# Tile norms in two parts an output apart, and requests in front of a tile's sums in GpSimd's queue

## The chip, the cores and the metric

The kernel runs on one core of a Trainium2 chip. The metric is the device time of one execution in microseconds (us); of a kernel that was run several times the median is given. The engines are TensorE (PE in the profile, its weight loads PEld), VectorE (DVE), ScalarE (ACT), GpSimd (POOL) and SyncE (SP). Each works off its own queue in order, and they wait for each other through semaphores.

## The reference, cut to what matters

Two layers of a gated transformer block on x of shape (4, 512, 256), all in float32. Each layer adds gated cross attention to a context and then a gated feed-forward part. Layer 0 has attention with a time decay and a feed-forward part with ternary weights. Layer 1 has attention with ReLU projections and then a feed-forward part with four experts, and that last part is where the change lies:

```
x = x + tanh(g_xattn[0]) * L0_attention(layernorm(x), ctx)
x = x + tanh(g_ffn[0])   * L0_ffn(layernorm(x))
x = x + tanh(g_xattn[1]) * L1_attention(layernorm(x), ctx)
x = x + tanh(g_ffn[1])   * L1_ffn(layernorm(x))

def L1_ffn(t):                       # t: (2048, 256)
    expert = argmax(t @ W_router)    # one of 4 for each token
    h = gelu(t @ W1[expert] + b1[expert])          # (2048, 1024)
    y = h @ Wo + bo + t
    return layernorm(y, eps=1e-12) * ln_gamma + ln_beta
```

## The kernel before, in words

Attention, routing and the first feed-forward part are worked in units whose order a small planner writes out; all of that stays as it is. The 2048 tokens of the last part are sorted by expert into 16 tiles of 128 tokens, so that a tile needs the weights of one expert only (the last three tiles, 13 to 15, mix two experts each and need two). The lists that say which token goes to which tile are made four times, each time with more of the batch routed: list 2 gives tiles 9 to 12, the mixed list tiles 13 to 15. The instructions that make a list run mostly on VectorE, with a collection on TensorE (`pidT`, line 999, then `pid`, line 1008) and a memset on GpSimd (`tid`, line 959) between them.

The code that the change touches runs after the last attention unit, at about 706 us. For each tile j:

- `fetch_rows(j)` (line 1037) and `fetch_weights(j)` (line 1053) are indirect transfers that GpSimd requests: the tile's 128 token rows, normed and not normed side by side (`xr`, 512 floats a row), and about 1 MB of expert weights (`wg`). A request needs the token or weight numbers of the list, and a free place in its pool.
- `turn_tile(j)`, "t j" in the queue below (line 1065): two transposes on TensorE, copied out by ScalarE.
- `hidden_half(j, f2, k)`, "h j" (line 1090): the hidden products on TensorE, GELU on ScalarE (line 1116); in the mixed tiles a second pass with other weights and a masked copy on VectorE (line 1106).
- `output_tile(j)`, "o j": y = row + bias on VectorE (line 1282), eight products into `pyf` on TensorE (line 1285), y = y + pyf on VectorE (line 1289).
- `norm_tile(j)`: statistics on VectorE (lines 1294, 1296, 1299), the power -1/2 of the variance on GpSimd (`rstd_y`, line 1300), a first multiply on VectorE (line 1301), three small instructions that refine the power (lines 1302 to 1306), and the last multiply and add (line 1307).
- `put_tile(j)` (line 1312): an indirect transfer, requested by GpSimd, that writes the tile's rows to their tokens' places in the output. Each put waits until the put before it has landed.

The order of all engines' queues in this part is the order in which the loop over `queue` calls these functions:

```
h4 o0 o1 o2 t5 o3 h5 t6 o4 h6 t7 o5 h7 t8 o6 h8 o7 t9 o8 t10 h9 h10 t11 o9 h11 t12 o10 h12
t13 o11 h13 t14 o12 h14 t15 o13 h15 o14 o15
```

`steps` hangs the making of list 2 and of the mixed list onto entries of it: after o1 the transposes of the last batch's routing, after o2 its products, after o3 its logits, after h5 ranks and list 2 up to `row_d`, after o4 the selections (`sel_d`, line 986) and weight rows, after o5 the collection, after h7 the tokens (line 1014) and a first part of the mixed list (`mixes`), after o6 and h8 two more, after o7 the mixed places, after o8 the mixed tiles (with the memset), after h9 the mixed selections, after h10 their collection, after o9 the mixed tokens. In each entry the order was: products; the steps; for an output its norm and the put of the tile before; and then the requests of `rows_at` and `weights_at`.

Of the kernel before, what the change touches and what calls it, by code (L numbers as in the profile page):

```python
# [11 lines left out]
F32 = mybir.dt.float32  # L12
U32 = mybir.dt.uint32
AF = mybir.ActivationFunctionType
ALU = mybir.AluOpType
# [4 lines left out]
P = 128  # L20
B, S, D = 4, 512, 256
H, DK = 16, 16
NT = S // P
# [8 lines left out]
TT = B * NT  # L32
# [19 lines left out]
def flamingo_kernel(ctx: ExitStack, tc: tile.TileContext, t: dict, out: bass.AP):  # L52
    nc = tc.nc
# [7 lines left out]
    sml = ctx.enter_context(tc.tile_pool(name="sml", bufs=4))  # L61
    ps = ctx.enter_context(tc.tile_pool(name="ps", bufs=8, space=PSUM))

    def bank_psum(name):
        return ps.tile([P, 512], F32, tag="bank", name=name)
# [36 lines left out]
    bo0, b20, bo1, gam1, bet1 = (rows[:, i, :] for i in range(5))  # L102
# [6 lines left out]
    def weight_place(name):  # L109
        return wts.tile([P, NC * FF + NF], F32, tag="wff", name=name)  # L110
# [21 lines left out]
    act = att.__enter__()  # L132
# [895 lines left out]
    xg, wg = {}, {}  # L1028

    def fetch_rows(j):  # L1030

        have = max(n for n, first in LISTS if first <= j or n == LISTS[0][0]) * S
        if j in (3, *range(LISTS[1][1], TT)) and made["behind"]:
            xg[j] = act.tile([P, 2 * D], F32, tag="xr", name=f"xr{j}", bufs=5)
        else:
            xg[j] = wts.tile([P, 2 * D], F32, tag="xg", name=f"xg{j}", bufs=4)
        nc.gpsimd.indirect_dma_start(  # L1037
            out=xg[j], out_offset=None, in_=rows_d[0:have, :],
            in_offset=bass.IndirectOffsetOnAxis(ap=token[:, j : j + 1], axis=0),
            bounds_check=have - 1, oob_is_err=False,  # L1040
        )


    def weights_of(j):
        return (j,) if j < T_ONE else (2 * j - T_ONE, 2 * j - T_ONE + 1)

    def fetch_weights(j):

        if j < T_AHEAD or (j - T_AHEAD) % 5 < 2:
            wg[j] = weight_place(f"wg{j}")  # L1050
        else:
            wg[j] = act.tile([P, NC * FF + NF], F32, tag="wg", name=f"wg{j}", bufs=3)
        nc.gpsimd.indirect_dma_start(  # L1053
            out=wg[j], out_offset=None, in_=t["w1e"],
            in_offset=bass.IndirectOffsetOnAxis(ap=wrow[:, j : j + 1], axis=0),
            bounds_check=NE * P - 1, oob_is_err=False,
        )

    made["behind"] = False
    xs, hs, ys, biases = {}, {}, {}, {}  # L1060
# [9 lines left out]
    def hidden_half(j, f2, k=0):  # L1070


        w1 = wg[weights_of(j)[k]]
        w = w1[:, 0 : NC * FF].rearrange("p (c f) -> p c f", c=NC)
        b1 = w1[:, NC * FF :]
        if j < T_AHEAD:
            ha = wts.tile([P, S], F32, tag="h", name=f"ha{j}{f2}", bufs=8)
            if f2 == 0:
                biases[j] = sml.tile([P, NF], F32, tag="b1", name=f"b1_{j}")
                nc.gpsimd.tensor_copy(biases[j], b1)  # L1080
        else:
            ha = act.tile([P, S], F32, tag="ha", name=f"ha{j}{f2}{k}", bufs=8)
            biases[j] = b1
        ha = ha.rearrange("p (f n) -> p f n", n=P)
        if k == 0:
            hs[j, f2] = ha
        ph = bank_psum(f"pg{j}{f2}{k}").rearrange("p (f n) -> p f n", n=P)
        for f in range(NF // 2):
            for c in range(NC):
                nc.tensor.matmul(  # L1090
                    ph[:, f, :], lhsT=w[:, c, ts(f2 * NF // 2 + f, P)], rhs=xs[j][:, c, :],
                    start=(c == 0), stop=(c == NC - 1),
                )
        if j < T_AHEAD:
            (nc.scalar.copy if j < T_AHEAD - 1 else nc.vector.tensor_copy)(ha, ph)
        else:
            activated(j, f2, ph, ha)
        if k == 1:

            m = j - T_ONE  # L1100
            if f2 == 0:
                masks[m] = act.tile([P, P], U32, tag="mask", name=f"mask{m}")
                nc.vector.tensor_scalar(
                    masks[m], made["from_one"], lim[:, m : m + 1], None, ALU.is_gt
                )
            nc.vector.copy_predicated(
                hs[j, f2], masks[m].unsqueeze(1).to_broadcast([P, NF // 2, P]), ha
            )
# [141 lines left out]
    for u in range(-NT, n_units):  # L1250
# [22 lines left out]
        if u in totals:  # L1273
            job, i = totals[u]
# [2 lines left out]
    assert not any(c["steps"] for c in chains), [c for c in chains if c["steps"]]  # L1277


    def output_tile(j):  # L1280
        y = ys[j] = act.tile([P, D], F32, tag="y", name=f"y{j}", bufs=4)
        nc.vector.tensor_tensor(y, xg[j][:, 0:D], bo1, ALU.add)
        py = bank_psum(f"pyf1_{j}")[:, 0:D]
        for f in range(NF):
            nc.tensor.matmul(  # L1285
                py, lhsT=hs[j, f // 4][:, f % 4, :], rhs=wo1[f // 4][:, f % 4, :],
                start=(f == 0), stop=(f == NF - 1),
            )
        nc.vector.tensor_tensor(y, y, py, ALU.add)

    def norm_tile(j):
        y = ys[j]
        st = sml.tile([P, 6], F32, tag="st", name=f"st_y{j}")
        nc.vector.bn_stats(st, y)
        mv = sml.tile([P, NT, 2], F32, tag="mv", name=f"mv_y{j}")
        nc.vector.bn_aggr(mv[:, 0, :], st)

        var, rstd, fix = (sml.tile([P, NT], F32, tag=v, name=f"{v}_y{j}") for v in ("var", "rstd", "fix"))
        nc.vector.tensor_scalar(var[:, 0:1], mv[:, 0, 1:2], 1e-12, None, ALU.add)
        nc.gpsimd.tensor_tensor(rstd[:, 0:1], var[:, 0:1], power[:, 0:1], ALU.pow)  # L1300
        nc.vector.scalar_tensor_tensor(y, y, mv[:, 0, 0:1], gam1, ALU.subtract, ALU.mult)
        nc.vector.scalar_tensor_tensor(
            fix[:, 0:1], rstd[:, 0:1], var[:, 0:1], rstd[:, 0:1], ALU.mult, ALU.mult
        )
        nc.vector.tensor_scalar(fix[:, 0:1], fix[:, 0:1], -0.5, 1.5, ALU.mult, ALU.add)
        nc.vector.tensor_tensor(rstd[:, 0:1], rstd[:, 0:1], fix[:, 0:1], ALU.mult)
        nc.vector.scalar_tensor_tensor(  # L1307
            y, y, rstd[:, 0:1], xg[j][:, D : 2 * D], ALU.mult, ALU.add
        )

    def put_tile(j):
        nc.gpsimd.indirect_dma_start(  # L1312
            out=out.rearrange("b s d -> (b s) d"),
            out_offset=bass.IndirectOffsetOnAxis(ap=token[:, j : j + 1], axis=0),
            in_=ys.pop(j), in_offset=None, bounds_check=B * S - 1, oob_is_err=False,
        )
# [5 lines left out]
    for f2 in range(2):  # L1322
# [5 lines left out]
    act = ctx.enter_context(tc.tile_pool(name="moe", bufs=2))  # L1328
# [12 lines left out]
    steps = {  # L1341
        ("o", 1): [turn3], ("o", 2): [products3], ("o", 3): [logits3],
        ("h", 5): [ranks3, lists, token_places, by_tile], ("o", 4): [*sels, by_expert],
        ("o", 5): [collected], ("h", 7): [tokens, mixes[0]], ("o", 6): [mixes[1]],
        ("h", 8): [mixes[2]], ("o", 7): [mixed_places], ("o", 8): [mixed_tiles],
        ("h", 9): mixed_sels, ("h", 10): [mixed_collected], ("o", 9): [mixed_tokens],
    }
# [9 lines left out]
        queue.insert(queue.index(place), item)  # L1357
    queue += [("o", TT - 2), ("o", TT - 1)]

    rows_at = {("h", 4): [6], ("o", 0): [7], ("o", 1): [8], ("o", 6): [9, 10], ("o", 7): [11]}  # L1360
    weights_at = dict(rows_at)
    for j in range(8, TT - 4):
        rows_at["o", j] = [j + 4]
    weights_at |= {
        ("o", 8): [12, 13], ("o", 9): [14], ("o", 10): [15], ("h", 12): [16], ("o", 11): [17],
        ("h", 13): [18],
    }
    for kind, j in queue:
        if kind == "h":
            for k in range(len(weights_of(j))):  # L1370
                for f2 in range(2):
                    hidden_half(j, f2, k)
        elif kind == "t":
            turn_tile(j)
        else:
            if j < 3:
                for f2 in range(2):
                    activated(j + 1, f2)
            output_tile(j)
        for job in steps.pop((kind, j), ()):  # L1380
            job()
        if kind == "o":
            norm_tile(j)
            if j > 0:
                put_tile(j - 1)
        for i in rows_at.pop((kind, j), ()):
            fetch_rows(i)
            if i in weights_at.get((kind, j), ()):
                fetch_weights(i)
        for i in weights_at.get((kind, j), ()):  # L1390
            if i not in wg:
                fetch_weights(i)
    put_tile(TT - 1)
    assert not steps


# [73 lines left out]
```

## Time and profile before

| what | value |
|---|---|
| median of 3 runs | 847.55 us (846.2 to 848.15) |
| the profiled execution | 847.92 us, its span 845.8 us |
| TensorE (PE) busy | 811.0 us, 96% of the span |
| VectorE (DVE) busy | 569.1 us, 67% |
| ScalarE (ACT) busy | 422.2 us, 50% |
| GpSimd (POOL) busy | 270.9 us, 32% |
| mean granted TensorE clock | 0.991 |

The span runs from the first to the last instruction of the profiled execution; 2.1 us of its time lie around it. In a row of the timeline stand the start in us from the span's start, the time that the row took, engine and line, the operation, what it writes and reads, a count, and in brackets how long the engine sat idle before it and what ended that wait. A wait for several semaphores is put down to the one that came last in the profile, which need not be the one that mattered. Rows of the waits give the engine and line that waited, what ended it, the sum in us, how often, and the longest.

### The profile page before, as it was taken

How to read it: one execution, taken by the hardware profiler on the slowest of the kernel's cores; microseconds unless marked ns; L12 is line 12 of the kernel's file. 1: busy time of each engine (PE TensorE's matmuls, PEld its weight loads, DVE VectorE, ACT ScalarE, POOL GpSimd, SP SyncE). 2: the span in 40 equal slices, each digit the busy share in tenths (PEclk: the TensorE clock that was granted, in tenths of full speed). 3: DMA queues.
4: the chain of work that ended last, by engine and by line, in shares of the span. 5: the costliest groups of instructions: out<-in, count | busy, mean ns of one | idle time of the engine just before them, and what ended most of it. 6: DMA issues, size and time to landing. Idle time of an engine off the chain costs nothing. (4 is left out here: it accounts for less than half of the span.)

```text
span 845.8 us, 13576 instructions
## 1 busy us (share of the span) xinstructions
PE 811.0 (96%) x5220; PEld 452.4 (53%) x5220; DVE 569.1 (67%) x1272; ACT 422.2 (50%) x884; POOL 270.9 (32%) x439
## 2 busy tenths in 40 slices
PE   6999999999999999999999999999999999898994
PEld 3444444535464345544474444554545557787993
DVE  6768868766857776568737676558688654786443
ACT  2475555653645453455426474346556667332341
POOL 5536445524333243321101120002103314526522
PEclk9999999999999999999999999999999999999997
DMA  8200000000001000000000010000104422707730
GB/s 314 68 1 1 1 1 1 2 1 1 1 1 38 1 1 1 1 26 1 1 1 26 1 46 6 1 1 1 51 2 150 144 96 89 255 13 243 258 138 19
DMA packets 17712, 42.27 MB, mean 50 GB/s; under 512 B 2033, under 2 KB 12017, under 8 KB 15217
## 3 DMA queue, kind: packets, MB, share of 16 engines
q0 software_dynamic: 5104, 27.34, 9.3%
q1 hardware_dynamic: 12128, 13.54, 4.7%
q8 instruction: 41, 0.67, 0.3%
q10 hardware_dynamic: 416, 0.54, 0.2%
q14 instruction: 23, 0.18, 0.1%
HBM read 35.13 MB, written 6.29 MB: 49 GB/s over the span
## 5 line engine op out<-in xcount | busy, mean ns | idle before, releaser
L512 DVE TENSOR_REDUCE m<-pm 128x1 f32<-128x512 f32 x512 | 316.7, 681 | 109.0 <-PE psc L498 106.5
L527 ACT ACTIVATE p<-psc 128x512 f32<-128x512 f32 x512 | 267.1, 602 | 151.8 <-PE psc L498 149.4
L498 PE MATMUL psc<-q,k 32*128 32x512 f32 x1024 | 278.7, 623 | 0.2 <-DVE h L676 0.2
L498 PE MATMUL pm<-k,q 32*128 32x512 f32 x1024 | 262.7, 616 | 1.5 <-ACT q L485 0.9
L530 POOL TENSOR_TENSOR p<-p,dec 128x256 f32<-128x256 f32 x128 | 93.7, 736 | 178.7 <-ACT p L527 178.7
L498 PEld LDWEIGHTS pm<-k,q 32*128 32x128 f32 x1024 | 92.9, 184 | 84.1 <-issue 50.2
L498 PEld LDWEIGHTS psc<-q,k 32*128 32x128 f32 x1024 | 106.3, 184 | 52.0 <-issue 25.9
L555 PE MATMUL po<-p,v 128*32 128x512 f32 x1024 | 116.5, 595 | 1.9 <-DVE m L512 1.9
L555 PEld LDWEIGHTS po<-p,v 128*32 128x32 f32 x1024 | 31.7, 109 | 81.8 <-issue 60.8
L1090 PE MATMUL pg<-xs,wg 128*128 128x128 f32 x608 | 71.6, 276 | 0.4 <-DVE m L512 0.4
L1090 PEld LDWEIGHTS pg<-xs,wg 128*128 128x128 f32 x608 | 69.8, 192 | 3.8 <-DVE m L512 1.4
L623 POOL TENSOR_TENSOR x<-x,o 128x256 f32<-128x256 f32 x14 | 10.2, 727 | 174.4 <-DVE o L616 131.7
L1116 ACT ACTIVATE ha<-pg,wg 128x128 f32<-128x128 f32 x120 | 34.2, 368 | 53.0 <-PE pg L1090 53.0
L668 PE MATMUL ph<-xTf,w1q 128*128 128x512 f32 x128 | 60.0, 605 | 0.0
L1285 PE MATMUL pyf<-wo,ha 128*128 128x256 f32 x256 | 59.3, 387 | 0.0
L383 PE MATMUL py_f<-w2q,h 128*128 128x256 f32 x256 | 57.2, 381 | 0.0
L561 ACT COPY oT<-po 128x512 f32<-128x512 f32 x32 | 18.7, 584 | 77.1 <-PE po L555 77.1
L383 PEld LDWEIGHTS py_f<-w2q,h 128*128 128x128 f32 x256 | 48.0, 190 | 9.3 <-DVE m L512 3.0
L1285 PEld LDWEIGHTS pyf<-wo,ha 128*128 128x128 f32 x256 | 48.7, 195 | 6.4
L455 PE MATMUL pk<-cT,wk 128*128 128x512 f32 x68 | 35.3, 644 | 7.2 <-DMA cT<-in_ctxT_dram 7.2
L668 PEld LDWEIGHTS ph<-xTf,w1q 128*128 128x128 f32 x128 | 22.6, 189 | 30.4 <-issue 18.2
L388 DVE SCALAR_TENSOR_TENSOR x<-py_f,tg,x 128x512 f32<-128x512 f32 x8 | 6.0, 751 | 42.8 <-PE py_f L383 42.8
(256 smaller groups left out, 816.5 us busy)
## 6 DMA issues: line engine op xcount, KB each, us to landing
x<-in_x_dram SPq DMA_DIRECT2D x4, 512.0 KB, 8.7
rows_d<-xn_f SPq DMA_DIRECT2D x4, 512.0 KB, 3.0
rows_d<-x SPq DMA_DIRECT2D x4, 512.0 KB, 3.4
cT<-in_ctxT_dram SPq DMA_DIRECT2D x3, 512.0 KB, 9.5
w1q<-in_w_dram SPq DMA_DIRECT2D x1, 1024.0 KB, 9.0
w2q<-in_w_dram SPq DMA_DIRECT2D x1, 1024.0 KB, 11.3
wo<-in_wo_dram SPq DMA_DIRECT2D x2, 512.0 KB, 3.8
rows<-in_rows_dram SPq DMA_DIRECT2D x1, 640.0 KB, 9.2
```

The lines of the kernel that those rows point to most:

```text
L383: nc.tensor.matmul(py[:, n, :], lhsT=operand(c, n0 + n), rhs=w[:, c, :], start=(c == 0), stop=(c == chunks - 1),)
L455: nc.tensor.matmul(pp, lhsT=attn_w[layer][w][:, c, ts(tt, P)], rhs=src[:, c, :], start=(c == 0), stop=(c == NC - 1),)
L498: nc.tensor.matmul(out_, lhsT=lhs[r, ts(n, P)], rhs=rhs[r, :], start=True, stop=True)
L512: nc.vector.tensor_reduce(m[:, n, 2 * pair + i, r : r + 1], pm[i], AX.X, ALU.max)
L527: nc.scalar.activation(p[:, i, :], psc[i], AF.Exp, scale=SCALE)
L530: nc.gpsimd.tensor_tensor(d, d, dec.unsqueeze(1).to_broadcast([P, 2, P]), ALU.mult)
L555: nc.tensor.matmul(po[i * HP : (i + 1) * HP, :], lhsT=v_sb[b % 2][0][:, kt, c0 : c0 + HP], rhs=ps_exp[NT * s + kt, i // 2][:, i % 2, :], s ...
L561: nc.scalar.copy(pos[s], po)
L668: nc.tensor.matmul(ph, lhsT=w1q[:, c, ts(f, P)], rhs=st["xT"][:, c, :], start=(c == 0), stop=(c == NC - 1),)
L1090: nc.tensor.matmul(ph[:, f, :], lhsT=w[:, c, ts(f2 * NF // 2 + f, P)], rhs=xs[j][:, c, :], start=(c == 0), stop=(c == NC - 1),)
L1116: nc.scalar.activation(ha[:, f, :], (ha if src is None else src)[:, f, :], AF.Gelu, bias=biases[j][:, fa : fa + 1],)
L1285: nc.tensor.matmul(py, lhsT=hs[j, f // 4][:, f % 4, :], rhs=wo1[f // 4][:, f % 4, :], start=(f == 0), stop=(f == NF - 1),)
```

## The change

`norm_tile` is cut in two. `sum_tile(j)` holds both additions, the statistics, the power and the first multiply; `norm_tile(j)` holds the refining and the last multiply. An output's entry now runs: products, then requests of rows and weights, then the steps, then `sum_tile(j)`, then `norm_tile(j - 1)` and `put_tile(j - 2)`. For the last two tiles the second part comes directly behind the first, with its own put; tile 13's second part and puts 12 and 13 come after h15. Before, both additions stood ahead of the entry's steps in VectorE's queue; now they stand behind them.

The requests move too: rows 9 are asked for right after the tokens of list 2 (in h7) and weights 9 ahead of them, rows 13 right after the mixed tokens (in o9), and all others ahead of their entry's sum, so ahead of its power and put in GpSimd's queue. The pool of rows has 7 places instead of 5, that of y 5 instead of 4.

```diff
-            xg[j] = act.tile([P, 2 * D], F32, tag="xr", name=f"xr{j}", bufs=5)
+            xg[j] = act.tile([P, 2 * D], F32, tag="xr", name=f"xr{j}", bufs=7)
...
     def output_tile(j):
-        y = ys[j] = act.tile([P, D], F32, tag="y", name=f"y{j}", bufs=4)
-        nc.vector.tensor_tensor(y, xg[j][:, 0:D], bo1, ALU.add)
-        py = bank_psum(f"pyf1_{j}")[:, 0:D]
+        py = pys[j] = bank_psum(f"pyf1_{j}")[:, 0:D]
...
-        nc.vector.tensor_tensor(y, y, py, ALU.add)
-
-    def norm_tile(j):
-        y = ys[j]
+    def sum_tile(j):
+        y = ys[j] = act.tile([P, D], F32, tag="y", name=f"y{j}", bufs=5)
+        nc.vector.tensor_tensor(y, xg[j][:, 0:D], bo1, ALU.add)
+        nc.vector.tensor_tensor(y, y, pys.pop(j), ALU.add)
         st = sml.tile([P, 6], F32, tag="st", name=f"st_y{j}")
         nc.vector.bn_stats(st, y)
         mv = sml.tile([P, NT, 2], F32, tag="mv", name=f"mv_y{j}")
         nc.vector.bn_aggr(mv[:, 0, :], st)
...
         nc.vector.tensor_scalar(var[:, 0:1], mv[:, 0, 1:2], 1e-12, None, ALU.add)
         nc.gpsimd.tensor_tensor(rstd[:, 0:1], var[:, 0:1], power[:, 0:1], ALU.pow)
         nc.vector.scalar_tensor_tensor(y, y, mv[:, 0, 0:1], gam1, ALU.subtract, ALU.mult)
+        moments[j] = var, rstd
+
+    def norm_tile(j):
+        var, rstd = moments.pop(j)
+        fix = small_y(j, "fix")
...
-    rows_at = {("h", 4): [6], ("o", 0): [7], ("o", 1): [8], ("o", 6): [9, 10], ("o", 7): [11]}
-    weights_at = dict(rows_at)
-    for j in range(8, TT - 4):
-        rows_at["o", j] = [j + 4]
+    rows_at = {("h", 4): [6], ("o", 0): [7], ("o", 1): [8], ("o", 6): [10]}
+    weights_at = {("h", 4): [6], ("o", 0): [7], ("o", 1): [8], ("h", 7): [9], ("o", 6): [10]}
+    for j in range(7, 9):
+        rows_at["o", j] = weights_at["o", j] = [j + 4]
+    rows_at |= {("o", 10): [14], ("o", 11): [15]}
     weights_at |= {
-        ("o", 8): [12, 13], ("o", 9): [14], ("o", 10): [15], ("h", 12): [16], ("o", 11): [17],
+        ("h", 10): [13], ("o", 9): [14], ("o", 10): [15], ("h", 12): [16], ("o", 11): [17],
         ("h", 13): [18],
     }
+    steps["h", 7].insert(1, lambda: fetch_rows(9))
+    steps["o", 9].append(lambda: fetch_rows(13))
     for kind, j in queue:
...
             output_tile(j)
+        for i in rows_at.pop((kind, j), ()):
+            fetch_rows(i)
+        for i in weights_at.pop((kind, j), ()):
+            fetch_weights(i)
         for job in steps.pop((kind, j), ()):
             job()
         if kind == "o":
+            sum_tile(j)
+        if kind == "o" and 0 < j < TT - 2:
+            norm_tile(j - 1)
+            if j > 1:
+                put_tile(j - 2)
+        elif (kind, j) == ("h", TT - 1):
+            norm_tile(j - 2)
+            put_tile(j - 3)
+            put_tile(j - 2)
+        elif kind == "o" and j >= TT - 2:
             norm_tile(j)
-            if j > 0:
-                put_tile(j - 1)
-        for i in rows_at.pop((kind, j), ()):
-            fetch_rows(i)
-            if i in weights_at.get((kind, j), ()):
-                fetch_weights(i)
-        for i in weights_at.get((kind, j), ()):
-            if i not in wg:
-                fetch_weights(i)
-    put_tile(TT - 1)
+            put_tile(j)
```

More of the change, by code (lines that the diff above doesn't have):

```diff
@@ L1277, in flamingo_kernel @@
     assert not any(c["steps"] for c in chains), [c for c in chains if c["steps"]]
+    pys, moments = {}, {}
     def output_tile(j):
-        y = ys[j] = act.tile([P, D], F32, tag="y", name=f"y{j}", bufs=4)
-        nc.vector.tensor_tensor(y, xg[j][:, 0:D], bo1, ALU.add)
-        py = bank_psum(f"pyf1_{j}")[:, 0:D]
+        py = pys[j] = bank_psum(f"pyf1_{j}")[:, 0:D]
         for f in range(NF):
@@ L1288, in output_tile, with small_y @@
             )
-        nc.vector.tensor_tensor(y, y, py, ALU.add)
-    def norm_tile(j):
-        y = ys[j]
+    def small_y(j, v):
+        return sml.tile([P, NT], F32, tag=v, name=f"{v}_y{j}")
+    def sum_tile(j):
+        y = ys[j] = act.tile([P, D], F32, tag="y", name=f"y{j}", bufs=5)
+        nc.vector.tensor_tensor(y, xg[j][:, 0:D], bo1, ALU.add)
+        nc.vector.tensor_tensor(y, y, pys.pop(j), ALU.add)
         st = sml.tile([P, 6], F32, tag="st", name=f"st_y{j}")
@@ L1296, in norm_tile @@
         nc.vector.bn_aggr(mv[:, 0, :], st)
-        var, rstd, fix = (sml.tile([P, NT], F32, tag=v, name=f"{v}_y{j}") for v in ("var", "rstd", "fix"))
+        var, rstd = small_y(j, "var"), small_y(j, "rstd")
         nc.vector.tensor_scalar(var[:, 0:1], mv[:, 0, 1:2], 1e-12, None, ALU.add)
@@ L1307, in norm_tile @@
         nc.vector.scalar_tensor_tensor(
-            y, y, rstd[:, 0:1], xg[j][:, D : 2 * D], ALU.mult, ALU.add
+            ys[j], ys[j], rstd[:, 0:1], xg[j][:, D : 2 * D], ALU.mult, ALU.add
         )
```

## The prediction

> **What bounds the kernel now.** I read the stretches first, since the change touches only the last 127 us. Columns: length of the stretch, then busy time of each engine, granted clock, share of the transfer engines, GB/s.
>
> ```profile
> 718.96:779.50 60.54, 53.41 (x405) 47.32 (x403) 47.95 (x207) 18.93 (x65) 29.33 (x32) 0.97 0.48 168
> 779.50:833.60 54.10, 54.10 (x383) 50.85 (x379) 22.41 (x71) 19.93 (x70) 20.19 (x22) 1.00 0.47 167
> ```
>
> From 779.5 to 833.6 TensorE never stops: nothing that VectorE or GpSimd save there can shorten the time. From 719 to 779.5 TensorE idles 60.54 - 53.41 = 7.1 us. The waits of TensorE in this part name each idle stretch:
>
> ```profile
> PE ptx L1065 <- DVE under_d L936: 4.2, 1, 4.2
> PE prk L768 <- DVE onehot L760: 1.4, 1, 1.4
> PE plT L742 <- DVE xTf L376: 1.3, 1, 1.3
> PE pidT_d L999 <- DVE sel_d L986: 0.2, 1, 0.2
> ```
>
> The name behind the 4.2 us is only the last event before it; the timelines of TensorE and GpSimd show the true cause:
>
> ```profile
> 757.14 3.62 PE L1285 MATMUL pyf<-wo,ha 128*128 128x256 f32 x16
> 764.95 0.44 PE L1065 MATMUL ptx<-ident,xr 128*128 128x128 f32 x2 [4.20 <-DVE under_d L936]
> 765.23 5.31 PE L1285 MATMUL pyf<-wo,ha 128*128 128x256 f32 x16
> ```
> ```profile
> 759.23 0.73 POOL L1300 TENSOR_TENSOR rstd_y<-var_y,power 128x1 f32<-128x1 f32 x1 [7.07 <-DVE var_y L1299]
> 760.15 1.03 POOL L1312 DMA_INDIRECT out_dram<-y,token_of  x1 [0.20 <-issue]
> 761.48 1.04 POOL L1037 DMA_INDIRECT xr<-rows_d,token_of  x1 [0.30 <-issue]
> ```
>
> The turn of tile 9 needs xr9. VectorE had written its tokens at 752.1, but GpSimd waited 7.07 us for tile 6's variance, then did the power and put 5, and asked for xr9 only at 761.48; it landed about 3.4 us later. The output product after it took 5.31 instead of 3.62 us, because the clock fell:
>
> ```profile
> 765.00:767.00 2.00, 2.00 (x7) 1.64 (x8) 1.76 (x9) 0.37 (x1) 1.13 (x2) 0.57 0.83 308
> ```
>
> Last, VectorE's waits inside a norm and for the memset, and the end on GpSimd:
>
> ```profile
> 721.64 0.22 DVE L1302 SCALAR_TENSOR_TENSOR fix_y<-rstd_y,var_y 128x1 f32<-128x1 f32 x1 [0.48 <-POOL rstd_y L1300]
> 773.15 0.21 DVE L962 TENSOR_TENSOR tid_d<-ge_d 128x48 f32<-128x48 f32 x1 [2.02 <-POOL tid_d L959]
> 776.55 2.49 DVE L986 TENSOR_TENSOR sel_d<-from_one,row_d 128x512 f32<-128x512 f32 x4
> ```
> ```profile
> 835.30 0.73 POOL L1300 TENSOR_TENSOR rstd_y<-var_y,power 128x1 f32<-128x1 f32 x1 [1.74 <-DVE var_y L1299]
> 836.23 1.03 POOL L1312 DMA_INDIRECT out_dram<-y,token_of  x1 [0.20 <-issue]
> 839.47 0.98 POOL L1312 DMA_INDIRECT out_dram<-y,token_of  x1 [2.20 <-DMA out_dram<-y,token_of]
> ```
>
> No instruction is added or removed, so this is a sum of moved waits.
>
> **Units.** On VectorE a "sum" (y add, py add, stats, aggregate, variance, first multiply) runs from 718.96 to 720.69 plus 0.40 until the next can start: 2.13 us. A "norm" (three small ones, last multiply) is 721.64 to 722.68: 1.04. Between them before lay the power's round trip through GpSimd, 721.64 - 720.69 - 0.40 = 0.55 of dead time a tile (1.59 for tile 2, where put 0 and two requests stood ahead of the power). A request takes GpSimd 1.0 and the next follows 1.33 after; a power 0.73.
>
> **Early routing (o1 to h5).** The turn's copy xTf now comes before sum 1 and norm 0 leaves sum 0. VectorE: sum 0 from 718.96 to 721.09, xTf to 721.7; before it began at 723.54. So plT's 1.32 us of idling goes. Then sum 1 to 723.8, norm 0 to 724.9, sum 2 to 727.0, norm 1 to 728.0, the five instructions that end in onehot to 729.0 (733.4 before). TensorE reaches prk at 733.62 - 1.41 - 1.32 = 730.9, so the 1.41 goes too. TensorE now runs 2.7 us ahead. Powers keep up: xr7 and wg7 push rstd 0 to 722.6-723.4, norm 0 asks at 723.8.
>
> **List 2 and tile 9.** VectorE on: sum 3 to 731.1, norm 2 to 732.1, ranks to row_d (736.10 to 741.31 before, 5.2) to 737.3, selections and weight rows (2.95) to 740.3, sum 4 to 742.4, norm 3 743.5, sum 5 745.6, norm 4 746.6. TensorE's pidT comes at 745.1 - 2.7 = 742.4: selections are there. pid ends at 747.3, tokens on VectorE at 747.9 (before 752.1). GpSimd by then: rstd 5, put 3 (held until put 2 has landed, about 746.9), wg9 at 748.2, xr9 at 749.5 and xr10, wg10 to 753.2. xr9 has 758.0 - 749.5 = 8.5 us until its turn at 760.76 - 2.7; its median to landing is 3.5, a weight ahead of it takes 7.0. So the 4.2 us go, and with full speed 1.69 after it: TensorE is then 2.7 + 4.2 + 1.7 = 8.6 us ahead and reaches the second collection (pidT of the mixed list, 777.83 before) at 769.2.
>
> **What is late next.** That collection needs the mixed list's selections from VectorE. On from 747.35: tokens .28 and mixes 2.87 to 750.5, mixes 2.78 to 753.3, sum 6 755.4, norm 5 756.5, mixes 2.13 to 758.6, places 3.02 to 761.6, sum 7 763.7 (variance 763.4), norm 6 764.8, comparison 765.0. Now the memset of tid: GpSimd does rstd 7 at 763.5, put 5 at 764.4, xr12 at 765.8, wg12 at 767.1, memset 768.1 to 768.65 (before too it ended 5.2 after the power began: 767.95 to 773.12). VectorE arrives at 765.0 instead of 1.6 after the power's end, so it waits 3.7 instead of 2.02. Then the rest of the list (0.69) to 769.4, sum 8 771.5, norm 7 772.5, four selections (0.63 each) 773.2 to 775.05. TensorE waits from 769.2 and ends the collection at 775.5 instead of 779.52: **4.0 us** of the 8.6 are left. Were the memset hidden it would be 7.6; were each VectorE step slower by 1%, 0.5 less. I take 4.0, range 2.5 to 5.5.
>
> **The clock.** Row: one stall of 4.2 us cost 1.69 in the product behind it. [...] I take the row, 1.7, and 0 to 3.4 as ends. With nothing else, TensorE stands 4.0 - 1.7 = **2.3** ahead for good, since the second stretch has no idle time to give.
>
> **Requests that wait inside GpSimd's queue.** wg9 to wg18 wait for earlier tiles' products; wg18 still waits for h13's first half with rstd 12 behind it, 10 us before that is wanted. xr13 waits for the mixed tokens (pid at about 779.5) with rstd 9 behind, whose variance comes 2 us later. xr13's turn is 15 us off. Seven row buffers and five of y: xr11 takes xr5's place (norm 5, done at 756.5, request at 757.5); y5 takes y0's, whose put has long landed. Cost 0; without that cover each would hold a power and then VectorE by its own lateness. The page's 27 MB of requests are the same.
>
> **The end.** Now put 13 goes at about 829.7 (before the shift) behind its norm, and put 14 directly after norm 14 ends at 833.5, not behind rstd 15 at 836.23. It lands 2.5 later, at 836.1. Norm 15 ends at 837.18, so put 15 goes at 837.3 instead of 839.47: **2.1 us**. If a put takes up to 6.1 to land (the longest), 0; if instant, 2.2.
>
> **Sum.** 2.3 + 2.1 = 4.4 us. Profiled execution 847.92, its span 845.8, 2.1 around it: 841.4 of span, **843.5** us. The median of the runs is 847.55, 0.4 below that execution.
>
> **Rivals.** (1) The selections don't hold TensorE: if the memset came early, VectorE kept up and the gate stayed open, 8.6 + 2.1 = 10.7: 837.2. For it: VectorE is busy 47.95 of 60.54, so it has room. Against: its own order of steps, above, arrives 6 us after TensorE. [...] (3) Slower: GpSimd's queue. Every request in front of a power and of the memset adds to VectorE's chain in order, then to TensorE's stall. The price is one for one from the memset at 768.65; it decides when the memset ends later than 768.65 + 4.4 = 773.1, that is when put 5, xr12 or wg12 is held 4.4 us by a landing (xr12 waits for wg9's, asked 17 us before). If held 7 us: 850.5. Against: in the trace of before only put 2 (2.79) waits over 0.7 us for a landing in this stretch, and none of the fetches. (4) No effect: the stall just changes place and the end too; 847.6. Against: the last put's 2.20 us has a plain cause.
>
> **Chances.** My sum with its ends (840 to 845.5) 0.68; (1) 0.10; (2) 0.10; (3) 0.08; (4) 0.04. A run of this kernel can tell 0.2%, 1.7 us. Faster: 0.68 + 0.10 + most of (2) = 0.85; same: (4) and the rest of (2), 0.06; slower 0.09. Range 839.5 to 846.5; that leaves out (1), (3) and some of (2).
>
> **What would show it.** Right: no idle before plT, prk and the turn of tile 9; xr9 asked near 749.5, ahead of rstd 6; one TensorE idle of about 4 us before pidT near 769, released by sel_d; VectorE waiting 3 to 4 us for tid's memset; the last put with no wait for a landing over 0.3. Wrong: TensorE idle elsewhere after 775, a norm that waits for its power, or a memset later than 770.

## The result

| | median | runs |
|---|---|---|
| before | 847.12 us | 6, 846.2 to 848.15 |
| changed | 843.97 us | 6, 841.69 to 844.27 |

The ratio is 0.9955, with a 95% interval of 0.9945 to 0.9965: 3.0 to 4.7 us faster. The forecast was 843.5.

The two profiled executions lie further apart, 847.92 and 841.69 us. Of that, 1.42 us stands ahead of the code that was changed: the first output product begins at 711.20 before and at 709.78 after. So I compare from that product on. From it to the end of the span are 845.8 - 711.20 = 134.6 us before and 839.6 - 709.78 = 129.8 after, 4.8 us less. All comparisons of profiles below are made in this way, and called "the tail".

**The stretches after** (length, busy time of TensorE, its weight loads, VectorE, ScalarE, GpSimd, granted clock, transfers). The borders are the same events as before, the start of sum 0 and the end of the mixed collection and of the last product:

```profile
717.55:774.00 56.45, 52.02 (x405) 46.39 (x404) 46.71 (x202) 18.81 (x65) 29.81 (x33) 0.96 0.57 201
774.00:829.36 55.36, 55.36 (x380) 51.77 (x379) 23.73 (x76) 19.93 (x70) 18.98 (x21) 0.98 0.40 144
```

The first stretch is 56.45 instead of 60.54 us, 4.1 shorter. The second is 1.3 longer with the same work at a mean clock of 0.98. TensorE's idle time has fallen from 7.1 to 4.4 us, and it is now a single wait:

```profile
PE pidT_d L999 <- DVE sel_d L986: 4.4, 1, 4.4
```

The timeline of TensorE shows it, and that the turn of tile 9 (756.01) and the product behind it run without a break:

```profile
756.01 0.38 PE L1065 MATMUL ptx<-ident,xr 128*128 128x128 f32 x2
756.23 3.62 PE L1285 MATMUL pyf<-wo,ha 128*128 128x256 f32 x16
...
759.90 7.31 PE L1090 MATMUL pg<-xs,wg 128*128 128x128 f32 x64
771.64 2.37 PE L999 MATMUL pidT_d<-sel_d,tid_d 128*32 128x128 f32 x32 [4.42 <-DVE sel_d L986]
...
774.41 4.65 PE L1285 MATMUL pyf<-wo,ha 128*128 128x256 f32 x16
```

The product that runs slowly (4.65 instead of 3.62) is now the one behind the mixed collection. Upstream of it, GpSimd and VectorE:

```profile
761.71 0.73 POOL L1304 TENSOR_TENSOR rstd_y<-var_y,power 128x1 f32<-128x1 f32 x1 [3.85 <-DVE var_y L1303]
762.65 1.06 POOL L1322 DMA_INDIRECT out_dram<-y,token_of  x1 [0.20 <-issue]
764.01 1.03 POOL L1037 DMA_INDIRECT xr<-rows_d,token_of  x1 [0.30 <-PE pg L1090]
765.34 0.99 POOL L1053 DMA_INDIRECT wg<-in_w1e_dram,wrow  x1 [0.31 <-issue]
766.33 0.54 POOL L959 MEMSET tid_d<- 128x512 f32 x1
```
```profile
763.02 0.21 DVE L954 TENSOR_TENSOR ge_d<-place_d,tiles_of 128x64 f32<-128x64 f32 x1
766.90 0.21 DVE L962 TENSOR_TENSOR tid_d<-ge_d 128x48 f32<-128x48 f32 x1 [3.67 <-POOL tid_d L959]
...
770.81 2.48 DVE L986 TENSOR_TENSOR sel_d<-from_one,row_d 128x512 f32<-128x512 f32 x4
```

VectorE reaches the comparison at 763.02 and stands still until the memset is done, which is the fifth thing in GpSimd's queue from power 7 on. The end, on GpSimd:

```profile
829.50 1.04 POOL L1322 DMA_INDIRECT out_dram<-y,token_of  x1 [1.45 <-DVE y L1317]
831.02 0.73 POOL L1304 TENSOR_TENSOR rstd_y<-var_y,power 128x1 f32<-128x1 f32 x1 [0.48 <-DVE var_y L1303]
833.21 1.04 POOL L1322 DMA_INDIRECT out_dram<-y,token_of  x1 [1.45 <-DVE y L1317]
```

The last put waits for its own norm (1.45 us) and no longer for the landing of the put before it. From the end of the last product to the end of the span it is 10.25 us, against 12.17.

### The profile page after: what moved, and what is told of

Its sections match the earlier page's. It is cut to its first block, busy times and chain, and to the rows that moved or that the text cites. A ratio compares the mean times of both kernels' runs of the same rounds, so it can differ in the third digit from the quotient of the medians.

```text
span 839.6 us, 13573 instructions
## 1 busy us (share of the span) xinstructions
PE 809.5 (96%) x5220; PEld 452.3 (54%) x5220; DVE 568.7 (68%) x1272; ACT 422.1 (50%) x884; POOL 270.3 (32%) x439
```

## The experiments

The theory to be tested: a chain of VectorE's steps, held last by GpSimd's memset, decides when TensorE can go on; the early requests for rows 9 in themselves bring nothing; two more microseconds come from the last puts; the clock takes some back. The chief rival: the gain is that of the moved requests. In the diffs, only what differs is shown. Four of the versions ran on one chip beside 13 runs of the kernel before, the other four on a second chip beside 16; each ratio is to the runs before on its own chip. On the first of these chips the first output product comes about 2 us later (711.7 to 711.9 in three profiles of changed versions, 709.8 to 709.9 on the second chip), so the tails compare better across the two than the times.

**The requests alone**: the norms stay whole, the requests are placed as in the changed kernel, with its lists and its seven places for rows.

```diff
             output_tile(j)
+        for i in rows_at.pop((kind, j), ()):
+            fetch_rows(i)
+        for i in weights_at.pop((kind, j), ()):
+            fetch_weights(i)
         for job in steps.pop((kind, j), ()):
             job()
         if kind == "o":
             norm_tile(j)
```

> The new places of the requests (and seven row places) on the old norms. My theory: the wait for tile 9's rows (4.2 us) and the slow product behind it go, but VectorE's chain to the mixed selections keeps its old length, so TensorE stands still before their collection instead, from about 772 to 776.5 and in part to 779. Nothing is gained, and the clock falls there: 847 to 848.6, same as before or up to 1.5 slower. Rival (the moved request for rows 9 is what gained): 4.2 + 1.7 faster than before, about 841.

Measured: 1.003 of before, 1.0019 to 1.0042. It is slower, and the interval lies just above what the theory gave (847 to 848.6 beside 847.12 is a ratio of 1.000 to 1.002); the rival's 0.993 is excluded. TensorE in its profile:

```profile
762.80 0.38 PE L1065 MATMUL ptx<-ident,xr 128*128 128x128 f32 x2
763.02 3.62 PE L1285 MATMUL pyf<-wo,ha 128*128 128x256 f32 x16
...
779.82 2.37 PE L999 MATMUL pidT_d<-sel_d,tid_d 128*32 128x128 f32 x32 [5.81 <-DVE sel_d L986]
```
```profile
PE plT L742 <- DVE xTf L376: 2.8, 1, 2.8
```

Tile 9 is turned without a wait, and all of the time so won, and more, is lost at two places: before `plT`, where TensorE waits 2.8 us instead of 1.3, and before the collection. What I had not foreseen: the collection ends later than before, 70.3 us after the first output product instead of 68.3. The waits on VectorE say why. With a whole norm, requests in front of the power are paid by VectorE itself:

```profile
723.86 0.22 DVE L1302 SCALAR_TENSOR_TENSOR fix_y<-rstd_y,var_y 128x1 f32<-128x1 f32 x1 [2.00 <-POOL rstd_y L1300]
```

Before, this wait of tile 0 was 0.48. It is the requests for tile 7 (two, 1.3 us from one to the next) that the power now follows. Up to the collection VectorE's waits for powers add up to 6.4 us instead of 5.2, and its wait for the memset is 2.3 instead of 2.0. That is 1.5 of the 2.0 us; the rest is not traced.

**The split norms alone**: the requests come where they came before, behind the put; the pools, the split and the end as in the changed kernel.

> The split norms and the new end, with the requests in their old places behind the put (pools as in the changed kernel). My theory: the turn of tile 9 waits about 3 us again, but that lies inside the time in which TensorE would wait for the mixed selections anyway; GpSimd's power 7, put, two requests and memset are as many as in the changed kernel, so the selections come at the same time. About the changed kernel's time or up to 1.5 less, since neither of two shorter stalls need let the clock fall: 842.5 to 844.2. Rival (requests gained): the wait for rows 9 costs 4 to 6 us again: 847 to 849.

Measured: 0.9919 of before, 0.9906 to 0.9933. That is more than I had expected (842.5 to 844.2 beside 847.12 is 0.9945 to 0.9966). Some of it may be the clock: eight of the 13 runs before on this chip have a mean granted clock of 0.989 or 0.990, the six of this version 0.991 to 0.997. The tail is 128.8 us, 5.8 less than before. So the split and the new end give the whole gain, and the rival is refuted a second time. What came together with the split, the additions behind the entry's steps and the larger pools, was not tried apart. The changed kernel had 0.9955 (0.9945 to 0.9965) in the first comparison and 0.995 (0.9938 to 0.9962) when it was run again on the second chip (below). Since this version did not run beside it, that the moved requests make the kernel slower is likely but not shown by the times alone; the profiles' tails say 128.8 us here and 129.8 with them. TensorE in its profile:

```profile
761.31 0.69 PE L1065 MATMUL ptx<-ident,xr 128*128 128x128 f32 x2 [3.15 <-DMA xr<-rows_d,token_of]
761.79 4.75 PE L1285 MATMUL pyf<-wo,ha 128*128 128x256 f32 x16
...
774.04 0.93 PE L999 MATMUL pidT_d<-sel_d,tid_d 128*32 128x128 f32 x16
```

The wait for the rows is back, 3.15 us, and the slow product with it. But the selections arrive at the same place in the tail as in the changed kernel (the collection ends 64.4 us after the first output product, against 64.2), and TensorE reaches them just in time. One stall has merely been exchanged for the other. The difference is in what comes behind: here the slow product lies in front of the collection, where TensorE had time to lose; in the changed kernel it lies behind it, where it has none.

**The memset early**: in the changed kernel, the mixed list's memset moves from `by_tile`, behind the requests for tile 12, to the entry h8.

```diff
-            tid = space("tid").rearrange("p (k w) -> p k w", w=HP)
-            nc.gpsimd.memset(tid, 0.0)
-            st["tid"] = tid
-            tid = tid[:, 0:K, 0:T]
+            if "tid" not in st:
+                clear_tid()
+            tid = st["tid"][:, 0:K, 0:T]
...
-        ("h", 8): [mixes[2]], ("o", 7): [mixed_places], ("o", 8): [mixed_tiles],
+        ("h", 8): [mixed_clear, mixes[2]], ("o", 7): [mixed_places], ("o", 8): [mixed_tiles],
```

`mixed_clear` is `clear_tid`, which takes the place and clears it.

> The changed kernel with the mixed list's memset on GpSimd moved from behind the requests for tile 12 to the entry h8, ahead of the requests for tile 11. My theory: VectorE's wait of 3.67 us for it goes, the selections end 3.7 earlier, TensorE's stall before the collection falls from 4.4 to under 1 us, and the clock stays up (1.5): 3.7 to 5.1 less than the changed kernel, about 839 to 840. Rival (VectorE's work, or something else, holds the collection): within 1 us of the changed kernel.

Measured: 0.9895 of before, 0.9879 to 0.9911. TensorE at the collection:

```profile
772.23 0.94 PE L1002 MATMUL pidT_d<-sel_d,tid_d 128*32 128x128 f32 x16 [1.88 <-DVE sel_d L989]
```

The stall is 1.9 us instead of 4.4, not under 1 as I had written: the collection ends 2.8 us earlier in the tail (61.45 after the first output product), not 3.7. VectorE reached the comparison 0.7 us later in the tail than in the changed kernel (53.9 instead of 53.2), and still stood idle for 0.46 us behind it; why is not shown. The output products on both sides of the stall took 3.62 us each (at 759.36 and 774.57). The tail is 125.8 us, 4.0 less than the changed kernel. So the memset was what ended last on VectorE's side, and behind it is VectorE's own order of steps.

**TensorE kept busy**: nine products that nobody reads, between h10 and the collection of the changed kernel.

```diff
-        ("h", 9): mixed_sels, ("h", 10): [mixed_collected]
+        ("h", 9): mixed_sels, ("h", 10): [fill, mixed_collected]
```

> The changed kernel with nine products of 0.38 us, whose result nobody reads, put on TensorE between h10 and the mixed collection: they fill 3.4 us of its 4.4 us stall. It adds work and removes no wait. [...]

If the lower clock is what makes the collection and the product behind it slow, the forecast was about 842.5; if they are slow for another reason, the changed kernel's 844.

Measured: 0.9938 of before, 0.9918 to 0.9958. That is below the changed kernel's 0.9955 and 0.995, but the intervals overlap, and the chips differ: by the times alone this is open. The profile is plain. The filling takes 4.05 us, somewhat more than the 3.4 I had reckoned with:

```profile
768.94 4.05 PE L1344 MATMUL fill<-wo,ident 128*128 128x256 f32 x18
```

The stretches from the end of h10 to the mixed `pid`, in the changed kernel and then with the filling:

```profile
769.00:771.60 2.60, 0.00 (x0) 0.00 (x0) 2.43 (x9) 0.00 (x0) 1.80 (x2) 0.63 0.53 215
771.60:774.00 2.40, 2.36 (x33) 0.91 (x34) 1.69 (x3) 0.00 (x0) 1.90 (x2) 0.50 0.51 106
774.00:776.00 2.00, 2.00 (x7) 1.73 (x7) 0.00 (x0) 0.64 (x2) 0.28 (x1) 0.50 0.78 296
776.00:779.00 3.00, 3.00 (x14) 2.51 (x14) 0.00 (x0) 0.00 (x0) 0.00 (x0) 0.92 0.99 367
```
```profile
769.00:773.80 4.80, 3.99 (x19) 3.20 (x19) 4.35 (x16) 1.14 (x4) 1.83 (x3) 1.00 0.66 220
773.80:776.00 2.20, 1.76 (x33) 0.76 (x34) 1.66 (x3) 0.00 (x0) 1.73 (x2) 1.00 0.36 90
```

With the filling the granted clock stays at 1.00. The collection ends at the same place in the tail (64.27 against 64.22, since the selections set it), and from its end to the mixed `pid` it takes 3.66 instead of 4.90 us. So the fallen clock costs 1.2 us in this execution, and work without any use makes the tail shorter, 128.6 instead of 129.8. The clock on record with each run points the same way: none of the twelve runs of the changed kernel has a mean above 0.993, three of the six with the filling have 0.994 to 0.997.

**The changed kernel again**, beside the next three on one chip.

> The changed kernel once more, so that the others of this chip can be set against it: 0.9945 to 0.9965 of before, as in the first comparison. The runs of norms and fill gave 0.992 and 0.994 of their before on another occasion; if the changed kernel is above 0.994 here too, the gate's 1.5 us is what parts them.

Measured: 0.995 of before, 0.9938 to 0.9962. Its profile repeats the first one: one stall of 4.5 us, a tail of 130.05 us.

**The end undone**: the last puts as before.

```diff
             put_tile(j - 3)
-            put_tile(j - 2)
         elif kind == "o" and j >= TT - 2:
             norm_tile(j)
-            put_tile(j)
+            put_tile(j - 1)
+    put_tile(TT - 1)
```

> The changed kernel with the last three puts as before: put 13 behind norm 14, put 14 behind norm 15, then put 15. My theory: put 15 waits again for put 14 to land, about 2 us more than the changed kernel. Rival (the last put's wait is hidden by what the core does after it): same time.

Measured: 0.9976 of before, 0.9967 to 0.9985, against 0.995 of the changed kernel on the same chip. The medians are 844.82 and 842.7: 2.1 us. GpSimd at the end:

```profile
832.83 1.04 POOL L1322 DMA_INDIRECT out_dram<-y,token_of  x1 [0.20 <-issue]
836.07 0.97 POOL L1322 DMA_INDIRECT out_dram<-y,token_of  x1 [2.19 <-issue]
```

The last request waits 2.19 us again, and the end behind the last product is 12.17 us, as before the change. In this profile the stall before the collection is 5.2 us instead of 4.4, though nothing ahead of it was changed: the collection ends 65.0 us after the first output product, against 64.2. By so much a single profile can be off.

**Memset early and selections ahead of sum 8**: besides the early memset, the four selections move up.

```diff
-        ("h", 8): [mixed_clear, mixes[2]], ("o", 7): [mixed_places], ("o", 8): [mixed_tiles],
-        ("h", 9): mixed_sels, ("h", 10): [mixed_collected], ("o", 9): [mixed_tokens],
+        ("h", 8): [mixed_clear, mixes[2]], ("o", 7): [mixed_places], ("o", 8): [mixed_tiles, *mixed_sels],
+        ("h", 10): [mixed_collected], ("o", 9): [mixed_tokens],
```

> The early memset, and the four mixed selections in entry o8 ahead of sum 8 and norm 7 on VectorE. In memset_early TensorE still waited 1.9 us for the first selection and twice 0.2 between them. My theory: VectorE's order of steps is what is left of the stall, so it goes: about 2 us less than memset_early, 0.987 of before. Rival (something else ends that wait, or sum 8 coming later holds a bank or GpSimd's queue): the same as memset_early, 0.9895.

Measured: 834.75 us, 0.9858 of before, 0.9844 to 0.9872, with the expected 0.987 inside. The waits of TensorE in the tail are empty. Its timeline:

```profile
759.97 7.31 PE L1093 MATMUL pg<-xs,wg 128*128 128x128 f32 x64
767.21 1.08 PE L1002 MATMUL pidT_d<-sel_d,tid_d 128*32 128x128 f32 x32
...
768.50 3.62 PE L1288 MATMUL pyf<-wo,ha 128*128 128x256 f32 x16
```

The collection follows the hidden products at once. The tail is 122.9 us: 6.9 less than the changed kernel, 11.7 less than before. This version beats both kernels, by 0.9% and 1.4%.

**Split norms, old requests, early memset.**

> The split norms with the requests in their old places, and the early memset. In norms TensorE waited 3.1 us for tile 9's rows, ran the product behind it slowly, and then hardly waited for the selections. My theory: the two stalls stood one behind the other, and the rows now decide, so the early memset gives nothing here, 0.5 us at most: 0.991 to 0.993 of before. So the moved requests are worth 2 to 3 us once the memset is early, and nothing while it is late. Rival (the rows' wait was harmless): the early memset gives 3 us or more here too, 0.988.

Measured: 0.993 of before, 0.9917 to 0.9942, as expected. Its profile:

```profile
PE ptx L1068 <- DMA xr<-rows_d,token_of: 3.8, 1, 3.8
```

This is now TensorE's only wait in the tail, which is 128.4 us, hardly less than the 128.8 of the split norms alone. The early memset gives 0.4 us here and 4.0 with the moved requests. In this profile rows 9 were asked for 0.6 us later in the tail than with the split norms alone (46.8 instead of 46.2), so it may be worth up to 1.0 (my estimate, 0.4 + 0.6). So the two need each other: as long as either the rows or the memset is late, TensorE stands still once.

## Why the prediction was right

**Early routing**: right. TensorE no longer waits for xTf or onehot; both lines are gone from its waits, 2.7 us as worked out. By `prk` TensorE was 3.1 us ahead in the tail and by the mixed collection 9.2, not 8.6; since the selections set when that ends, this changed nothing. Powers kept up: VectorE waits for one only at the last two tiles (0.9 us in all).

**List 2 and tile 9**: right. xr9 was asked for at 748.88 in a tail that is 1.4 us early (749.5 was predicted, so 748.1), ahead of power 6 at 753.24, and its turn did not wait.

**What is late next**: right, and closest. The wait for the memset was 3.67 us (3.7 predicted, 2.02 before), and the end of the collection came 4.1 us earlier in the tail (4.0). That it agrees to 0.1 is in part luck: VectorE came to the comparison 0.6 us and to the end of the selections 0.3 us earlier than reckoned, and the collection, at a granted clock of 0.50, gave that back. It ended 0.7 us behind the last selection, where 0.45 was reckoned and with the filling, at a granted clock of 1.00, the eight products that wait for the last selection took 0.43.

**The clock**: that it falls at the new stall too was right, and the price was taken too large. The gate, in the prediction and in the expectation of the repeat, stands for what lowers this granted clock. I took the row's 1.7 us; the filling shows 1.2 (4.90 - 3.66). By the rows of the filling's section the clock was at 0.50 from 769.7 to 776.5. Until 774.0 that cost hardly anything, since TensorE stood still and then waited for the selections; from there on 2.5 us were left, and half of that is 1.25, against 1.2 measured. And before the change all 3.4 us of it, from 765.3 to 768.7, lay on work: 1.7. The clock fell 2.5 us after TensorE had stopped at 767.2 and stayed down for 6.8 us; before the change it fell 4.5 us after the stop at 760.8 and stayed down for 3.4. What sets these times is not shown. The range of 0 to 3.4 held, but no run shows its upper end: measured are 1.7 before the change and 1.2 after it. What was left out is that part of the low clock can lie in the stall itself, where it cost hardly anything.

**Requests inside GpSimd's queue**: their cost was put at 0, and no power that had requests in front of it was late for VectorE. That this rests on the split is what the requests alone showed: there the same order costs VectorE 1.5 us at tile 0. One wait was overlooked, that for the memset of list 2, which stands in GpSimd's queue behind a put that was held for 3.79 us by the landing of the put before (it goes at 733.79, the memset at 734.84). VectorE waited 0.52 us for it, and between 0 and 1.5 us in the other profiles with split norms. TensorE waited for list 2 in none of them; how much of it reaches the mixed selections is not shown.

**The end**: 2.1 predicted; 1.9 in the profiles, 2.1 in the medians.

**The sum**: 4.1 - 1.3 + 1.9 = 4.7 by what was measured, 4.8 in the tails, 4.4 predicted, and 3.0 to 4.7 in the runs. That 843.5 came within 0.5 us of the median is in part luck: the sum was taken off the profiled execution, 847.92, while the median of the runs before is 847.12; taken off that it gives 842.7.

What separates the tails' 4.8 from the 3.15 between the medians goes with the clock. The changed kernel's runs fall into two groups in both comparisons (841.7 to 842.3 and 843.4 to 844.3), and the profiled executions come from the lower one. The mean granted clock of each run is 0.993 throughout the lower group and 0.989 throughout the upper. The runs before beside the repeat part in the same way, 846.1 to 847.3 at 0.992 or 0.993 and 847.7 to 848.4 at 0.990 or 0.991. Lower against lower the medians there are 846.7 and 841.9, upper against upper 848.0 and 843.7: 4.8 and 4.3 us, on both sides of the predicted 4.4. In the first comparison four of the six changed runs are of the upper group, and their median with them. Where in those runs the clock fell is not on record; in the trace of the kernel before it was also at 0.50 from 28.0 to 31.4 us after the start, where that of the changed kernel shows 1.00, which goes with the 1.42 us ahead of the tail.

**The rivals**: that the selections don't hold TensorE was refuted by its 4.4 us wait, and the last version but one shows what it would have been worth, 834.75. That the queue of GpSimd makes the kernel slower did not happen, but does when the norms are whole. That the end alone gains was refuted: it is 2 of the 4.8. No effect is excluded by the interval. The chances that go with them don't quite add: what (4) and the rest of (2) come to is 0.07 and (3) is 0.08, where 0.06 and 0.09 stand.

## What to carry to other kernels

A stall that is taken away is worth only as much as the time to the next one: before costing it at its full length, follow the other engines to the next place at which they meet. When a request is moved forward in a queue, look for what stands behind it there, above all small things like a memset or a power, whose consumer has no slack; these go ahead of the requests. An instruction that waits for a round trip through another engine is best cut behind the question, with other work put before the answer is needed.

## What the runs showed of the hardware

In these runs a stall's price depended on where it lay as well as on its length: two stalls of 3.15 and 4.42 us were each followed by a slow output product (4.75 and 4.65 instead of 3.62 us), but only the slow product behind the second stall, which nothing else held up, made the tail longer. The time lost to the lower clock was half of the part of it that fell on such work: 1.7 us of 3.4 before the change and 1.2 of 2.5 in the changed kernel. Products without any use, 4.05 us of them, held the granted clock at 1.00 and shortened the tail by 1.2 us in the profile.
